# Second cross-attention of a Perceiver kernel: projection pieces between a step's halves, a second junk buffer, one head's side matrix added on GpSimd

## The chip, the cores and the metric

The kernel runs on one core of one Trainium2 chip. The metric is the time of one execution on the device in microseconds (us). Before the change it is 2459.25 us, the median of 3 runs (2456.62 to 2461.36). Everything is float32.

A core has five engines with a queue of instructions each: TensorE (PE; its weight loads are shown apart as PEld), VectorE (DVE), ScalarE (ACT), GpSimd (POOL) and SyncE (SP), which here only issues DMAs. They wait for one another through semaphores.

## The reference

The network has four layers; each is a cross-attention, a self-attention and a feed-forward part on a state `x` of 128 rows x 256. The four cross-attentions (called l0x, l1x, l2x, l3x in the kernel) read the same context of 12,544 rows x 256. Only the second, l1x, is touched. Cut to what matters, it is

```python
x = x + _L1_xattn_ref(ctx_1024, ctx_1024, _layernorm(x), fside_SxS2_0, fside_BxS2_0, ...)

def _L1_xattn_ref(K_in, V_in, Q_in, mask_attn, mask_pad, ...):      # 16 heads of 16
    K = K_in @ Wk + bk                                              # 12544 x 256
    V = V_in @ Wv + bv
    Q = Q_in @ Wq + bq                                              # 128 x 256
    KQ = einsum('bhld,bhpd->bhlp', K, Q) / sqrt(16)
    KQ = KQ + mask_pad.reshape(b, 1, l, 1)
    KQ = KQ + mask_attn.T.reshape(1, 1, l, lp)                      # 128 x 12544, the side matrix
    alpha = softmax(KQ, axis=2)                                     # over the 12544 keys
    O = einsum('bhlp,bhld->bhpd', alpha, V)
    return O.transpose(0, 2, 1, 3).reshape(b, lp, 256) @ Wo + bo
```

So each head needs the scores of 128 queries against 12,544 keys, with a full matrix added to them (the same for all heads), and then a softmax over the keys. The side matrix exists in l1x alone (`side=True` in the kernel).

## The kernel before, in words

**Projections.** Keys and values of all four cross-attentions are computed in small pieces: 512 keys by 128 features (`keys`, L200) or 256 keys by 256 features (`values`, L214), about four or eight weight loads each. A piece's products land in one PSUM bank (L315), are evicted by ScalarE (L209 for keys; L232 for values while l1x runs) and written to DRAM by a DMA that GpSimd issues (L212, L237). From there key and value tiles are fetched again. The pieces stand in one list in the order of layers; `pump(n)` (L142) issues the next n of them. While l1x runs, its own remaining pieces are issued, and then those of l2x.

**Cross-attention** (`cross`, L355). The 16 heads are worked off in 4 groups of 4; a group has 25 tiles of 512 keys (the last has 256), so there are 100 tiles in all. The softmax is exact, so each tile is visited twice. The first visit computes the scores with queries on the partitions (`score_s`, products L483) and only takes their maximum: for l1x, VectorE adds the side matrix and takes the maximum in one instruction (L491), which must also write its elementwise result somewhere; that goes to a buffer `junk` that nobody reads (L489, one buffer). A second short instruction reads the accumulator into `mxs`. When a group's 25 tiles are done, the maximum is folded into the queries (`raised`, `lower`; L505 to L515). The second visit, 27 steps later (`lead`, L364), computes the scores with keys on the partitions (`score_t`, products L533), VectorE adds the transposed side matrix into an SBUF tile `e` (L541), ScalarE takes the exponential in place (L546), and TensorE multiplies with the values (`values`, L572, products L588; a column of ones gives the softmax's denominator). VectorE adds this sum to `acc` (L592, L594).

**The order.** The order of l1x is written out by hand (`manual_schedule`, L615), in steps `at`. A step fetches key, value and side tiles, computes the scores (L623), issues pieces (L632 to L637) and then the weighted sum of the *previous* step's tile (L640 to L649). The scores of a step come in two halves (L561): first the maxima of heads 2 and 3 with the exponentials of heads 0 and 1, then the maxima of heads 0 and 1 with the exponentials of heads 2 and 3. Four heads use four separate row groups of the TensorE array, which is why the two kinds are mixed. Within a half all products are issued first and all drains after them: the maxima, then per head the add and the exponential. For steps 0 to 26 there are maxima alone, for 27 to 99 both, for 100 to 126 exponentials alone, then in one half with all four heads.

PSUM has 8 banks; each tile of scores, each piece and each weighted sum takes the next one in turn (`bank`, L135), and waits until whatever was in it eight allocations before is drained. `e` has two buffers.

How many pieces a step issues is set by a `goal` (l1x's own pieces have to be ready in time) and by `rate`, which for l1x is (0.95, 0.0, 1.2, 1.2, 0.4) pieces a step for steps 2 to 26, 27 to 51, 52 to 76, 77 to 101 and from 102 on. Own value pieces come on top, two in each of the steps up to 44.

Of the kernel before, what the change touches and what calls it, by code (L numbers as in the profile page):

```python
# [12 lines left out]
AF = mybir.ActivationFunctionType  # L13
ALU = mybir.AluOpType
# [4 lines left out]
P = 128  # L19
# [6 lines left out]
NST = -(-S2 // ST)  # L26
# [51 lines left out]
class Net:  # L78
# [276 lines left out]
    def cross(self, name, side=False, project=True, rate=()):  # L355
# [4 lines left out]
        nc, tc = self.nc, self.tc  # L360
# [6 lines left out]
        with ExitStack() as es:  # L367
# [18 lines left out]
            for u in range(units):  # L386
                g, r = width * u // 4, rows(u)
                q = pool.tile([P, P], F32, name=f"{name}_qb{u}", tag=f"qb{u}")
# [10 lines left out]
            kt, vt, ft, gt, mxs, es_, acc = {}, {}, {}, {}, {}, {}, {}  # L399
# [70 lines left out]
            def score_s(k, heads):  # L470

                u, i = divmod(k, NST)
                s, m = i * ST, min(ST, S2 - i * ST)
                if u not in mxs:
                    mxs[u] = pool.tile([P, width, NST], F32, name=f"{name}_mxs{u}", tag="mxs",
                                       bufs=2)
                t, at = kt[u, s // SB], s % SB
                banks = {j: self.bank(f"{name}_s{k}_{j}") for j in heads}

                def products():  # L480
                    for j in heads:
                        r = tile_of(u, j)
                        nc.tensor.matmul(banks[j][:, :m], qb[u][r, :], t[r, at : at + m],  # L483
                                         start=True, stop=True)

                def drain():
                    for j in heads:
                        if side:
                            junk = ep.tile([P, ST], F32, name=f"{name}_j{k}_{j}", tag="junk",  # L489
                                           bufs=1)  # L490
                            nc.vector.tensor_tensor_reduce(  # L491
                                out=junk[:, :m], in0=banks[j][:, :m], in1=ft[k][:, :m], scale=1.0,
                                scalar=-3.0e38, op0=ALU.add, op1=ALU.max,
                                accum_out=mxs[u][:, j, i : i + 1])
                        else:
                            nc.vector.tensor_reduce(out=mxs[u][:, j, i : i + 1],  # L496
                                                    in_=banks[j][:, :m], axis=AX.X, op=ALU.max)
                return products, drain
# [19 lines left out]
            def score_t(k, heads):  # L518

                u, i = divmod(k, NST)  # L520
                s, m = i * ST, min(ST, S2 - i * ST)
                t, at = kt[u, s // SB], s % SB
                banks = {j: self.bank(f"{name}_t{k}_{j}") for j in heads}
                if k not in es_:
                    es_[k] = ep.tile([P, width, ST], F32, name=f"{name}_e{k}", tag="e",
                                     bufs=5 if width == 2 else 2)
                e = es_[k]

                def products():
                    for a in range(m // P):  # L530
                        for j in heads:
                            r = tile_of(u, j)
                            nc.tensor.matmul(banks[j][:, a * P : (a + 1) * P],  # L533
                                             t[r, at + a * P : at + (a + 1) * P], qb[u][r, :],
                                             start=True, stop=True)

                def drain():
                    for j in heads:
                        src = banks[j][:, :m]
                        if side:  # L540
                            nc.vector.tensor_tensor(  # L541
                                out=e[:, j, :m], in0=src,
                                in1=gt[k][:, : m // P, :].rearrange("p a q -> p (a q)"),
                                op=ALU.add)
                            src = e[:, j, :m]
                        nc.scalar.activation(e[:, j, :m], src, AF.Exp)  # L546
                return products, drain

            def scores(ke, km):

                if ke is None and km is None:
                    return
                heads = tuple(range(width))
                if ke is None:
                    sets = [[(score_s, km, heads)]]
                elif km is None:
                    sets = [[(score_t, ke, heads)]]
                elif width == 2:
                    sets = [[(score_s, km, heads), (score_t, ke, heads)]]
                else:  # L560
                    sets = [[(score_s, km, (2, 3)), (score_t, ke, (0, 1))],  # L561
                            [(score_s, km, (0, 1)), (score_t, ke, (2, 3))]]
                for part in sets:
                    parts = [make(k, heads) for make, k, heads in part]
                    for products, _ in parts:
                        products()
                    for _, drain in parts:
                        drain()
                if km is not None:
                    raised(km)  # L570

            def values(ks):  # L572


                u, i = divmod(ks[0], NST)
                ps = self.bank(f"{name}_p{ks[0]}")
                todo = []
                for k in ks:
                    s = (k - u * NST) * ST
                    m = min(ST, S2 - s)  # L580
                    v, at, e = vt[u, s // SB], (s % SB) // P, es_.pop(k)
                    for a in range(m // P):
                        for j in range(width):
                            c = 17 * (width * (at + a) + j)
                            todo.append(((width * a + j) % 4, v[:, c : c + 32],
                                         e[:, j, a * P : (a + 1) * P]))
                for n, (c, lhs, rhs) in enumerate(todo):
                    nc.tensor.matmul(ps[32 * c : 32 * c + 32, :P], lhs, rhs, start=n < 4,  # L588
                                     stop=n >= len(todo) - 4, skip_group_check=True)
                if i == 0:  # L590
                    acc[u] = self.small.tile([P, P], F32, name=f"{name}_at{u}", tag="at")
                    nc.vector.tensor_copy(acc[u], ps[:, :P])  # L592
                else:
                    nc.vector.tensor_tensor(out=acc[u], in0=acc[u], in1=ps[:, :P], op=ALU.add)  # L594
# [20 lines left out]
            with tc.manual_schedule():  # L615
                for k in (0, 1):
                    fetch_k(k)
                for at in range(total + lead + 3):
                    fetch_k(at + 2)
                    fetch_v(at + 2 - lead)  # L620
                    ke = at - lead if 0 <= at - lead < total else None
                    km = at if at < total else None
                    scores(ke, km)  # L623
                    if 0 < at <= total and at % NST == 0:
                        lower(at // NST - 1)


                    left = sum(1 for (n, _, _), _ in self.jobs if n == name)
                    goal = min(n_k, 2 * (at + 6))
                    if at >= lead - 6:  # L630
                        goal = min(n_own, n_k + 2 * (at - lead + 7))
                    self.pump(min(left, max(0, goal - (n_own - left))))  # L632
                    phase = max(0, at - 2) // NST
                    due += rate[phase] if phase < len(rate) else 0.0
                    while due >= 1.0:
                        self.pump(1)
                        due -= 1.0  # L637


                    while waiting:  # L640
                        u, i = divmod(waiting[0], NST)
                        n = NST - i if NST - i < 2 * batch else batch
                        last = waiting[0] + n - 1
                        if ke is not None and ke - last < behind - batch + 1:
                            break
                        if last > waiting[-1]:
                            break
                        values(waiting[:n])
                        waiting = waiting[n:]  # L649
                    if ke is not None:  # L650
                        waiting.append(ke)
                    u, i = divmod(at - lead - 2 - NST, NST)
                    if i == 0 and 0 <= u < units:
                        finish(u)
# [826 lines left out]
```

## Time and profile before

| | us |
|---|---|
| median of 3 runs | 2459.25 (2456.62 to 2461.36) |
| the profiled execution | 2463.49 |
| its span, first to last instruction | 2461.6 |
| TensorE products busy | 2324.9 (94%) |
| weight loads busy | 1716.3 (70%) |
| VectorE busy | 1628.7 (66%) |
| ScalarE busy | 1150.0 (47%) |
| GpSimd busy | 246.2 (10%) |
| l1x, from its first score product to its last weighted sum | 648.0 to 1300.3 |

The profile shows one execution. A row of the timeline or of a group names the source line (L533), the engine, the operation, what it writes and reads ("l1x_t<-l1x_qb,l1x_kt"), and the shape; "x8" is how many instructions a row stands for, and in brackets stands how long the engine was idle before it and which engine's work ended that. Rows of the timeline begin with start and length in us. Matmuls are pipelined and their ends are modelled, so a TensorE that is busy 99% is not a TensorE at its peak. Each float32 product shows as two matmul records.

### The profile page before, as it was taken

Reading aid. Unit: us, or ns where it says so; the run is one execution under the profiler, and the core shown is the slowest. Engines: PE = TensorE matmul, PEld = TensorE weight load, DVE = VectorE, ACT = ScalarE, POOL = GpSimd, SP = SyncE. Lnnn points to the kernel's source line nnn. Section 1 sums busy time; section 2 is a strip of 40 time slices with the busy share of each in tenths; the row PEclk is TensorE's granted clock in tenths of the full one; section 3 lists DMA queues with packets and bytes.
Section 4 is the critical chain, followed back from the end, with each engine's and each line's share of the span. In section 5 each row is a group of like instructions: output and inputs, shape, how many; then the busy total and the mean of one; then the engine's idle time right before and its main releaser. Section 6 shows DMA issues by size and latency. Waiting matters only on the chain. (4 is left out here: it accounts for less than half of the span.)

```text
span 2461.6 us, 75645 instructions
## 1 busy us (share of the span) xinstructions
PE 2324.9 (94%) x32103; PEld 1716.3 (70%) x32103; DVE 1628.7 (66%) x3503; ACT 1150.0 (47%) x2109; POOL 246.2 (10%) x465
## 2 busy tenths in 40 slices
PE   6999999999899999999998998899999679999969
PEld 3358888876447876666777744478888546888848
DVE  2566688522477788888886734788882769888331
ACT  2213366773214445545582254046668302666832
POOL 2221100001221100000101111200000121000001
PEclk9999999999999999999999998999999888999979
DMA  7766633237779867777765675553322633333216
GB/s 273 263 222 215 208 97 93 69 118 278 259 232 303 275 216 223 229 227 219 223 198 191 211 254 195 165 151 92 92 78 68 231 109 101 91 91 97 63 44 225
DMA packets 191119, 430.29 MB, mean 175 GB/s; under 512 B 26908, under 2 KB 83248, under 8 KB 186688
## 3 DMA queue, kind: packets, MB, share of 16 engines
q1 hardware_dynamic: 154576, 269.26, 36.9%
q0 software_dynamic: 35840, 154.94, 16.8%
q8 instruction: 256, 4.19, 0.7%
q10 hardware_dynamic: 368, 1.25, 0.1%
q14 instruction: 79, 0.65, 0.1%
HBM read 319.18 MB, written 106.16 MB: 173 GB/s over the span
## 5 line engine op out<-in xcount | busy, mean ns | idle before, releaser
L546 ACT ACTIVATE l1x_e<-l1x_e 128x512 f32<-128x512 f32 (+1 forms) x400 | 240.5, 622 | 248.2 <-DVE l1x_e L541 248.2
L491 DVE CUSTOM_DVE_ANT_0 l1x_j<-l1x_s,l1x_f 128x512 f32<-128x512 f32 (+1 forms) x400 | 271.1, 678 | 80.9 <-PE l1x_t L533 29.9
L496 DVE TENSOR_REDUCE l0x_mxs<-l0x_s 128x1 f32<-128x512 f32 (+1 forms) x400 | 244.3, 672 | 97.5 <-PE l0x_s L483 66.0
L546 ACT ACTIVATE l0x_e<-l0x_t 128x512 f32<-128x512 f32 (+1 forms) x400 | 203.2, 594 | 176.9 <-PE l0x_t L533 173.4
L546 ACT ACTIVATE l3x_e<-l3x_t 128x512 f32<-128x512 f32 (+1 forms) x400 | 203.4, 594 | 167.2 <-PE l3x_s L483 92.6
L496 DVE TENSOR_REDUCE l2x_mxs<-l2x_s 128x1 f32<-128x512 f32 (+1 forms) x400 | 243.8, 672 | 36.7 <-PE l2x_t L533 24.3
L546 ACT ACTIVATE l2x_e<-l2x_t 128x512 f32<-128x512 f32 (+1 forms) x400 | 203.4, 594 | 137.2 <-PE l2x_t L533 133.5
L496 DVE TENSOR_REDUCE l3x_mxs<-l3x_s 128x1 f32<-128x512 f32 (+1 forms) x400 | 243.4, 671 | 33.1 <-PE l3x_t L533 23.9
L541 DVE TENSOR_TENSOR l1x_e<-l1x_t,l1x_g 128x512 f32<-128x512 f32 (+1 forms) x400 | 249.9, 671 | 11.3 <-PE l1x_t L533 8.3
L483 PE MATMUL l3x_s<-l3x_kt,l3x_qb 32*128 32x512 f32 (+1 forms) x800 | 202.8, 652 | 7.1 <-DMA l3x_kt<-l3x_kx 3.5
L533 PE MATMUL l1x_t<-l1x_qb,l1x_kt 32*128 32x128 f32 x3136 | 204.3, 284 | 2.7 <-ACT l1x_vs L232 0.6
L483 PE MATMUL l1x_s<-l1x_kt,l1x_qb 32*128 32x512 f32 (+1 forms) x800 | 203.2, 618 | 3.4 <-DMA l1x_kt<-l1x_kx 3.2
L533 PEld LDWEIGHTS l1x_t<-l1x_qb,l1x_kt 32*128 32x128 f32 x3136 | 171.6, 187 | 36.5 <-ACT l2x_ks L209 19.6
L483 PE MATMUL l2x_s<-l2x_kt,l2x_qb 32*128 32x512 f32 (+1 forms) x800 | 189.5, 620 | 5.8 <-DMA l2x_kt<-l2x_kx 5.3
L483 PE MATMUL l0x_s<-l0x_kt,l0x_qb 32*128 32x512 f32 (+1 forms) x800 | 183.5, 614 | 5.6 <-ACT l0x_ks L209 3.8
L533 PE MATMUL l3x_t<-l3x_qb,l3x_kt 32*128 32x128 f32 x3136 | 181.1, 281 | 0.0
L533 PE MATMUL l2x_t<-l2x_qb,l2x_kt 32*128 32x128 f32 x3136 | 180.0, 280 | 0.0
L533 PE MATMUL l0x_t<-l0x_qb,l0x_kt 32*128 32x128 f32 x3136 | 178.9, 279 | 0.0
L533 PEld LDWEIGHTS l3x_t<-l3x_qb,l3x_kt 32*128 32x128 f32 x3136 | 160.8, 187 | 6.5 <-issue 5.0
L533 PEld LDWEIGHTS l2x_t<-l2x_qb,l2x_kt 32*128 32x128 f32 x3136 | 159.8, 186 | 5.9 <-issue 5.0
L533 PEld LDWEIGHTS l0x_t<-l0x_qb,l0x_kt 32*128 32x128 f32 x3136 | 159.1, 186 | 5.9 <-issue 5.0
L588 PEld LDWEIGHTS l1x_p<-l1x_e,l1x_vt 128*32 128x32 f32 x3136 | 82.0, 110 | 51.3 <-DVE l1x_mxs L491 18.9
(599 smaller groups left out, 3665.8 us busy)
## 6 DMA issues: line engine op xcount, KB each, us to landing
l1x_f<-in_fside SPq DMA_DIRECT2D x96, 256.0 KB
l1x_g<-in_fsideT SPq DMA_DIRECT2D x96, 256.0 KB
w<-in_w_l3f POOLq DMA_DIRECT2D x16, 1024.0 KB, 5.1
l0x_vx<-l0x_vs POOLq DMA_DIRECT2D x24, 544.0 KB, 5.5
l0x_vt<-l0x_vx SPq DMA_DIRECT2D x48, 272.0 KB
l1x_vx<-l1x_vs POOLq DMA_DIRECT2D x24, 544.0 KB, 5.9
l1x_vt<-l1x_vx SPq DMA_DIRECT2D x48, 272.0 KB
l2x_vx<-l2x_vs POOLq DMA_DIRECT2D x24, 544.0 KB, 4.8
```

Of the source, the lines that this page charges most:

```text
L483: nc.tensor.matmul(banks[j][:, :m], qb[u][r, :], t[r, at : at + m], start=True, stop=True)
L491: nc.vector.tensor_tensor_reduce(out=junk[:, :m], in0=banks[j][:, :m], in1=ft[k][:, :m], scale=1.0, scalar=-3.0e38, op0=ALU.add, op1=ALU.m ...
L496: nc.vector.tensor_reduce(out=mxs[u][:, j, i : i + 1], in_=banks[j][:, :m], axis=AX.X, op=ALU.max)
L533: nc.tensor.matmul(banks[j][:, a * P : (a + 1) * P], t[r, at + a * P : at + (a + 1) * P], qb[u][r, :], start=True, stop=True)
L541: nc.vector.tensor_tensor(out=e[:, j, :m], in0=src, in1=gt[k][:, : m // P, :].rearrange("p a q -> p (a q)"), op=ALU.add)
L546: nc.scalar.activation(e[:, j, :m], src, AF.Exp)
L588: nc.tensor.matmul(ps[32 * c : 32 * c + 32, :P], lhs, rhs, start=n < 4, stop=n >= len(todo) - 4, skip_group_check=True)
```

## The change

Three things change in l1x. The unread output of the maxima gets two buffers in place of one. The pieces of a step are counted before the scores, and half of them, rounded up, is issued between the two halves of the scores, where a step has both kinds; the rest comes, as before, after the scores (now behind `lower`). And head 3's scores of the second visit no longer get their side matrix from VectorE: ScalarE copies them from PSUM to `e`, GpSimd adds the side matrix there in place, and the exponential is not issued with the others but by `last_head`, which is called after the first half of the next step (or after its only half), or at the latest before the weighted sum that reads it.

```diff
                             junk = ep.tile([P, ST], F32, name=f"{name}_j{k}_{j}", tag="junk",
-                                           bufs=1)
+                                           bufs=2)
...
                 def drain():
                     for j in heads:
                         src = banks[j][:, :m]
+                        if side and j == 3:
+                            part = e[:, j, :m]
+                            nc.scalar.copy(part, src)
+                            nc.gpsimd.tensor_tensor(
+                                out=part, in0=part,
+                                in1=gt[k][:, : m // P, :].rearrange("p a q -> p (a q)"),
+                                op=ALU.add)
+                            late[k] = part
+                            continue
                         if side:
                             nc.vector.tensor_tensor(
                                 out=e[:, j, :m], in0=src,
...
-            def scores(ke, km):
+            late = {}
+
+            def last_head(k):
+                part = late.pop(k, None)
+                if part is not None:
+                    nc.scalar.activation(part, part, AF.Exp)
+
+            def scores(ke, km, between):
...
-                for part in sets:
+                for n, part in enumerate(sets):
+                    if n == 1:
+                        between()
                     parts = [make(k, heads) for make, k, heads in part]
                     for products, _ in parts:
                         products()
                     for _, drain in parts:
                         drain()
+                    if n == 0 and ke is not None:
+                        last_head(ke - 1)
                 if km is not None:
                     raised(km)
...
                 u, i = divmod(ks[0], NST)
+                for k in ks:
+                    last_head(k)
                 ps = self.bank(f"{name}_p{ks[0]}")
...
-                    scores(ke, km)
-                    if 0 < at <= total and at % NST == 0:
-                        lower(at // NST - 1)
                     left = sum(1 for (n, _, _), _ in self.jobs if n == name)
                     goal = min(n_k, 2 * (at + 6))
                     if at >= lead - 6:
                         goal = min(n_own, n_k + 2 * (at - lead + 7))
-                    self.pump(min(left, max(0, goal - (n_own - left))))
                     phase = max(0, at - 2) // NST
                     due += rate[phase] if phase < len(rate) else 0.0
-                    while due >= 1.0:
-                        self.pump(1)
-                        due -= 1.0
+                    pieces = min(left, max(0, goal - (n_own - left))) + int(due)
+                    due -= int(due)
+                    inner = (pieces + 1) // 2 if side and ke is not None and km is not None else 0
+                    scores(ke, km, lambda: self.pump(inner))
+                    if 0 < at <= total and at % NST == 0:
+                        lower(at // NST - 1)
+                    self.pump(pieces - inner)
```

## The prediction

> **What bounds the kernel now.** I read the busy table by stage first, to see where the second attention (l1x) spends its time, then the timeline of two kinds of step, then the list of waits. Each step handles one 512-key tile; its start is read in the timeline as the first weight load of its products. The busy table, cut at step starts (columns: window, its length, busy time and count of TensorE products, weight loads, VectorE, ScalarE, GpSimd, then granted clock, DMA share, GB/s):
>
> ```profile
> core 0: us, PE busy (x) PEld busy (x) DVE busy (x) ACT busy (x) POOL busy (x), PEclk, DMA share, GB/s
> 647.98:750.63 102.65, 96.56 (x390) 47.85 (x391) 75.02 (x219) 18.20 (x29) 22.96 (x35) 0.97 0.75 244
> ...
> 765.78:877.62 111.84, 111.84 (x1413) 94.06 (x1409) 86.26 (x208) 53.80 (x95) 15.54 (x32) 1.00 0.84 268
> 877.62:913.17 35.55, 35.06 (x502) 26.74 (x498) 32.71 (x88) 16.00 (x27) 1.72 (x3) 0.95 0.70 216
> 913.17:1212.03 298.86, 297.26 (x3681) 193.82 (x3677) 254.55 (x640) 149.43 (x252) 17.04 (x33) 0.99 0.72 224
> 1212.03:1296.63 84.60, 82.66 (x1735) 65.50 (x1732) 69.52 (x136) 68.10 (x118) 6.05 (x13) 1.00 0.62 196
> ```
>
> Row 1 is maxima only (27 steps), rows 2 to 4 both passes (16 steps with two pieces, 7 with one or none, 48 with one or two), row 5 the exponential pass alone (26). No engine is free by much: in row 4 VectorE is 85% busy, in row 5 VectorE and ScalarE are 82% and 80% busy. The order decides. A one-piece step of row 4 in the timeline:
>
> ```profile
> 1002.24 0.70 PE L483 MATMUL l1x_s<-l1x_kt,l1x_qb 32*128 32x512 f32 x2
> ...
> 1003.00 0.67 ACT L209 ACTIVATE l2x_ks<-l2x_k,cols 128x512 f32<-128x512 f32 x1
> ...
> 1003.40 0.69 DVE L491 CUSTOM_DVE_ANT_0 l1x_j<-l1x_s,l1x_f 128x512 f32<-128x512 f32 x1 [0.73 <-PE l1x_t L533]
> ...
> 1004.24 0.69 DVE L491 CUSTOM_DVE_ANT_0 l1x_j<-l1x_s,l1x_f 128x512 f32<-128x512 f32 x1
> ...
> 1004.86 1.28 DVE L541 TENSOR_TENSOR l1x_e<-l1x_t,l1x_g 128x512 f32<-128x512 f32 x2
> ...
> 1005.58 1.23 ACT L546 ACTIVATE l1x_e<-l1x_e 128x512 f32<-128x512 f32 x2 [1.91 <-DVE l1x_e L541]
> ...
> 1007.74 0.70 PE L483 MATMUL l1x_s<-l1x_kt,l1x_qb 32*128 32x512 f32 x2
> ```
>
> See the pitches: two maxima start 0.84 apart, but a maximum and the add behind it 0.62 apart. The 0.22 is the second maximum waiting for the first to release the single junk buffer (in the built program its wait names the accumulator read just ahead of it). VectorE's step is 2(0.84+0.62+0.60+0.60)+0.2 = 5.5 us; the row's steps average 298.86/48 = 6.23. What is lost beside it is seen in the waits of this row:
>
> ```profile
> PEld l1x_t L533 <- ACT l2x_ks L209: 19.6, 30, 0.9
> ```
>
> The key piece's eviction stands in ScalarE's queue behind the exponentials, and the next step's second half waits for that PSUM bank. A stretch of row 5, the exponential pass alone:
>
> ```profile
> 1287.15 1.17 PE L533 MATMUL l1x_t<-l1x_qb,l1x_kt 32*128 32x128 f32 x32
> ...
> 1288.40 2.48 DVE L541 TENSOR_TENSOR l1x_e<-l1x_t,l1x_g 128x512 f32<-128x512 f32 x4 [0.82 <-PE l1x_t L533]
> 1289.13 2.42 ACT L546 ACTIVATE l1x_e<-l1x_e 128x512 f32<-128x512 f32 x4 [0.67 <-DVE l1x_e L541]
> 1289.27 1.17 PE L533 MATMUL l1x_t<-l1x_qb,l1x_kt 32*128 32x128 f32 x32
> ...
> 1291.60 0.79 PEld L588 LDWEIGHTS l1x_p<-l1x_e,l1x_vt 128*32 128x32 f32 x26 [0.46 <-ACT l1x_e L546]
> ...
> 1292.59 1.17 PE L533 MATMUL l1x_t<-l1x_qb,l1x_kt 32*128 32x128 f32 x32
> ```
>
> The next tile's scores (1289.27) are issued before this tile's exponentials are done, so TensorE, VectorE and ScalarE work on different tiles at once: 84.60/26 = 3.25 us a step.
>
> **The change, part by part.** *Second junk buffer.* The 0.22 goes: a pair of maxima in each half-step, three gaps in a maxima-only step. In row 1 the maxima run back to back at 0.84, 3.36 us a step, and the waits of 650 to 704 us put 11.4 and 6.4 us of weight-load waits on the maxima. TensorE's own one-piece step there is 1.14+1.98 less 0.14 overlap = 2.98. At most the 15 steps from 650.2 to 704.0 us, now 3.59 long, fall to that (9 us); the key tiles' DMA waits and a DMA share of 0.75 take part back. I take -5, bounds -9 and 0.
>
> *Pieces between the halves.* The first half's evictions get time and the piece's eviction comes earlier in ScalarE's queue, so the L209 wait goes. The price: two halves no longer overlap. Together they take 2.03 unstalled; apart about 1.14 each less 0.07, so +0.18 (bounds 0 and 0.3). Two-piece steps of row 2 alternate 6.62 and 7.36 (mean 6.99); without the stall 6.62+0.18 = 6.80: 16 x -0.19 = -3. VectorE (5.5 less 0.44 for the gaps and 0.60 for head 3's add: 4.5) and the DMAs fit.
>
> *Head 3.* VectorE loses one add (0.60) a step, ScalarE gains a copy (0.55 from the L232 copies' pitch), GpSimd an add. ScalarE mixes copies and exponentials without table loads today. The GpSimd add has no near row: its only two-input add, 128x64, took 315 ns; scaled by elements that is 2.5 us, while memsets (206 ns for 128 columns, 978 for 1024) give 0.5 as floor. [...] But it has cover. In a one-piece step the second half starts at 2.98 us, its first maximum at 4.14, the second and the add 0.62 each later, head 2's exponential at 6.10, head 3's copy at 6.70 to 7.3; its result is called for at 10.3, in the next step (worked out below). So 3.0 us are free, more than either value; above 3.0 it would show.
>
> *Where head 3's exponential stands.* This decides. It is queued on ScalarE in the **next** step: behind the exponentials of heads 0 and 1 of that step, and, where the exponential pass is alone, behind heads 0, 1, 2 and the copy of head 3. The weighted sum (L588 before) of the old tile comes at the end of that same step on TensorE, and its fourth product waits for it. Behind that product stand the rest of the sum and all scores of the step after. So TensorE can no longer start step n+1 before ScalarE has worked through step n: a closed loop.
>
> Loop with both passes: scores to first maximum 1.16 (1002.24 to 1003.40); two maxima 1.24; add to exponential 0.72; three exponentials 0.60+0.60+0.63; to the sum 0.05; rest of the sum to the next scores 0.99 (1291.60 to 1292.59). Together 5.99 us, whether the step has one piece or none. With two, TensorE itself reaches the sum at about 6.0 us and doesn't wait: 6.80.
> Row 3: 7 x 5.99 less 0.2 for the short tile = 41.7 against 35.55: +6.
> Row 4: 38 x 5.99 + 10 x 6.80 + 1 for the two group changes = 296.6 against 298.86: -2. What the relief of VectorE gains is eaten by the loop.
>
> Loop of the exponential pass alone: 1.25 to the first add, 0.73 to the exponential, three exponentials 1.80, copy 0.55, last exponential 0.63, 0.05, rest of the sum 0.99: 6.00 against 3.25. A piece there (1.91) lies inside the wait. 26 x 6.00 less 0.8 for the short tile = 155.2 against 84.60: **+70.6**. The last tile is exposed at the end, with its GpSimd add: +2.
>
> Sum: -5 -3 +6 -2 +70.6 +2 = +69. The profiled execution took 2463.49 us (span 2461.6, 1.9 around it); with the change 2532. The median is 4.2 lower: 2459.25 + 69 = **2528 us**. The other stages keep their work.
>
> **Rivals.**
> *Faster: no loop.* If the late exponential came in time, both-pass steps would fall to TensorE's floor: one piece 2.03+1.98+1.08 less two overlaps of 0.07, and 0.18 for the split: 5.13; so row 4 becomes 38 x 5.13 + 68 + 1 = 264 (-35), row 3 7 x 4.5 = 31.5 (-4), row 5 ScalarE's 4 x 0.60 + 0.55 + a piece's copy in two steps of five (0.23) = 3.2 (-1); with -5 and -3 that is -48: 2411. For it speak VectorE's 85% and the L209 wait. Against it: the exponential would have to end within 4.0 us of a step's start (1.1 where the pass is alone), and the durations above give 4.95 and 4.96.
> *Loop only at the end.* With both passes the chain may be shorter than added up (a step of 5.3 instead of 5.99): 45 x -0.7 = -31: 2497. For it: three of its terms are pitches of back-to-back instructions. Against: the 1.16 and 0.72 are read off directly.
> *GpSimd too slow.* If its add takes 4.0 us, or waits behind a DMA issue in its queue, 38 one-piece steps grow by 1.0: 2566. For it: no row of that size. Against: both values lie below 3.0.
>
> **How the numbers follow.** Chances: my forecast 0.73, loop only at the end 0.10, slow GpSimd 0.12, no loop 0.05. 0.2% (5 us) is about what a measurement of this kernel can tell from no change. Slower: the first three but for a sliver, 0.93; same 0.02; faster 0.05. Range: the forecast's bounds (row 1 -4 to +5, row 2 -3 to +3, the two loops 0.3 a step over 71 steps) give 2505 to 2552; taking in the second rival's near half and part of the third's, 2500 to 2560.
>
> **What the profile after would show.** The maxima 0.62 apart in both places; L209 and L232 no longer named by the second half's weight loads; the fourth product of the weighted sum waiting on ScalarE's late exponential and starting 5.0 us after the step's first product, in every step but the two-piece ones; steps of 6.0 us from about 1210 on, with TensorE idle nearly half of them; that stage near 155 us. Wrong would be: steps near 3.3 there (no loop), or GpSimd's add as the last thing waited for.

## The result, and the profile after

The changed kernel takes 2546.23 us (median of 4 runs, 2543.98 to 2556.55); the kernel before took 2458.07 us beside it (4 runs, 2456.62 to 2461.36). The ratio is 1.0365 (95% interval 1.0333 to 1.0396): 3.7% slower. The forecast was 2528 us with a range of 2500 to 2560.

The profiled span grew from 2461.6 to 2546.3 us, by 84.7. The second attention, l1x, from its first score product to its last weighted sum, grew from 652.6 (648.0 to 1300.6) to 739.3 us, by 86.7; the stages around it give 2 back. So the whole loss is in l1x. Here is the forecast beside the measured times, in the stages of the prediction's rows (row 1 reaches here up to the start of row 2, so that it holds, behind the 27 steps with maxima alone, two steps with both passes):

| us | row 1, maxima | row 2, two pieces | row 3, one or none | row 4, both passes | row 5, exponentials alone | tail | sum |
|---|---|---|---|---|---|---|---|
| before | 117.80 | 111.84 | 35.56 | 298.85 | 84.61 | 3.98 | 652.6 |
| forecast | 112.8 | 108.8 | 41.7 | 296.6 | 155.2 | 6 | 721.1 |
| after | 112.92 | 113.05 | 44.37 | 292.07 | 169.93 | 6.96 | 739.3 |

The busy table of the changed kernel, rows 3, 4 and 5 of these stages (columns: window, its length, busy time and count of TensorE product records, weight loads, VectorE, ScalarE, GpSimd, granted clock, DMA share, GB/s):

```profile
874.84:919.21 44.37, 32.49 (x503) 25.73 (x499) 31.09 (x87) 20.02 (x38) 10.57 (x10) 0.84 0.57 180
919.21:1211.28 292.07, 279.17 (x3677) 183.39 (x3676) 221.09 (x584) 166.82 (x297) 77.77 (x82) 0.99 0.73 229
1211.28:1381.21 169.93, 112.50 (x1736) 85.26 (x1732) 56.57 (x110) 79.19 (x144) 39.16 (x41) 0.81 0.32 100
```

The last row has doubled, and no engine in it is near its capacity: TensorE is busy 66% of it, ScalarE 47%, VectorE 33%, GpSimd 23%. TensorE's 1736 product records (two for each product) are as many as before (1735) but are shown busy for 112.5 us instead of 82.7, at a granted clock of 0.81 instead of 1.00. In row 4 VectorE went from 85% to 76% busy, and the stage is only 2% shorter.

A one-piece step of row 4 (timeline; only the links of the path are shown):

```profile
1005.96 0.70 PE L483 MATMUL l1x_s<-l1x_kt,l1x_qb 32*128 32x512 f32 x2
...
1007.11 0.69 DVE L491 CUSTOM_DVE_ANT_0 l1x_j<-l1x_s,l1x_f 128x512 f32<-128x512 f32 x1 [0.76 <-PE l1x_t L533]
...
1007.73 0.69 DVE L491 CUSTOM_DVE_ANT_0 l1x_j<-l1x_s,l1x_f 128x512 f32<-128x512 f32 x1
...
1008.34 1.28 DVE L552 TENSOR_TENSOR l1x_e<-l1x_t,l1x_g 128x512 f32<-128x512 f32 x2
...
1009.06 1.23 ACT L557 ACTIVATE l1x_e<-l1x_e 128x512 f32<-128x512 f32 x2 [1.77 <-DVE l1x_e L552]
...
1010.20 0.61 ACT L565 ACTIVATE l1x_e<-l1x_e 128x512 f32<-128x512 f32 x1
...
1010.86 1.06 PE L612 MATMUL l1x_p<-l1x_e,l1x_vt 128*32 128x128 f32 x26 [0.37 <-ACT l1x_e L565]
...
1011.85 0.70 PE L483 MATMUL l1x_s<-l1x_kt,l1x_qb 32*128 32x512 f32 x2
```

This is the closed loop of the forecast, link by link. The two maxima are now 0.62 apart, not 0.84. Then the adds, two exponentials, head 3's late exponential (L565, of the *previous* tile) at 1010.20, the rest of that tile's weighted sum (L612) at once behind it, and the next step's scores behind that: 5.89 us. The forecast had 5.99.

Two steps of row 5, where the exponential pass is alone; the first starts at 1259.66, the second at 1266.36, the third at 1273.97:

```profile
1259.66 1.17 PE L533 MATMUL l1x_t<-l1x_qb,l1x_kt 32*128 32x128 f32 x32
...
1261.63 1.82 ACT L557 ACTIVATE l1x_e<-l1x_e 128x512 f32<-128x512 f32 x3 [2.54 <-DVE l1x_e L552]
...
1263.83 0.63 ACT L565 ACTIVATE l1x_e<-l1x_e 128x512 f32<-128x512 f32 x1
...
1264.51 1.92 PE L612 MATMUL l1x_p<-l1x_e,l1x_vt 128*32 128x128 f32 x26 [3.33 <-ACT l1x_e L565]
...
1266.36 2.09 PE L533 MATMUL l1x_t<-l1x_qb,l1x_kt 32*128 32x128 f32 x32
...
1268.52 1.89 DVE L552 TENSOR_TENSOR l1x_e<-l1x_t,l1x_g 128x512 f32<-128x512 f32 x3 [1.77 <-PE l1x_t L533]
...
1272.13 1.91 PE L612 MATMUL l1x_p<-l1x_e,l1x_vt 128*32 128x128 f32 x26 [3.10 <-ACT l1x_e L565]
...
1273.97 2.09 PE L533 MATMUL l1x_t<-l1x_qb,l1x_kt 32*128 32x128 f32 x32
```

Again the sum's rest waits for L565, and the next scores come behind the sum. But something is in it that the forecast didn't have. The same 32 records of score products take 1.17 us in the first step and 2.09 in the second, and the same 26 records of the sum take 1.92 us (1.06 in row 4's step above). The engine's rows of exactly these two steps, in the columns of the first table, say why:

```profile
1259.66:1266.36 6.70, 3.37 (x66) 2.49 (x65) 2.17 (x4) 2.83 (x5) 1.27 (x1) 0.80 0.15 43
1266.36:1273.97 7.61, 4.51 (x65) 3.33 (x65) 2.17 (x4) 2.83 (x5) 1.27 (x1) 0.50 0.26 71
```

The granted TensorE clock is 0.50 throughout the second step. Cut at its own changes, the clock around these steps reads:

```profile
1250.10:1256.90 6.80, 5.85 (x63) 4.77 (x64) 2.13 (x4) 2.01 (x4) 1.26 (x1) 0.50 0.47 140
1256.90:1263.70 6.80, 3.84 (x75) 2.60 (x73) 2.22 (x5) 4.26 (x9) 1.42 (x2) 1.00 0.37 134
1263.70:1277.40 13.70, 9.79 (x125) 7.66 (x126) 3.73 (x8) 4.12 (x8) 2.54 (x2) 0.50 0.22 60
```

In row 5 every stretch at half clock lasts 3.4 us or a multiple of it (6.8, 13.7). In the list of waits of row 5 (engine and line, what it waited for: us in total, times, longest) one line stands for nearly all that TensorE waits, the weight loads of the sum in each of the 26 steps:

```profile
PEld l1x_p L612 <- ACT l1x_e L565: 65.0, 26, 3.6
```

These waits differ. In the 14 steps in which TensorE has no projection piece to do, neither products nor weight loads run for 3.1 to 3.3 us; in the 12 steps with a piece for 0.2 to 1.4 us. Every stretch at half clock begins in a step without a piece, between 2.0 us into its wait and 0.5 us behind the end. A step with a piece is long (up to 6.8 us) where it begins in such a stretch.

### The profile page after: what moved, and what is told of

Its sections match the earlier page's. It is cut to its first block, busy times and chain, and to the rows that moved or that the text cites. A ratio compares the mean times of both kernels' runs of the same rounds, so it can differ in the third digit from the quotient of the medians.

```text
span 2546.3 us, 75819 instructions
## 1 busy us (share of the span) xinstructions
PE 2329.5 (91%) x32103; PEld 1719.7 (68%) x32103; DVE 1560.9 (61%) x3403; ACT 1189.2 (47%) x2209; POOL 371.1 (15%) x565
## 3 DMA queue, kind: packets, MB, share of 16 engines
q10 hardware_dynamic: 368, 1.25, 0.1%
## 5 line engine op out<-in xcount | busy, mean ns | idle before, releaser
L491 DVE CUSTOM_DVE_ANT_0 l1x_j<-l1x_s,l1x_f 128x512 f32<-128x512 f32 (+1 forms) x400 | 253.4, 677 | 122.1 <-PE l1x_t L533 83.9
L557 ACT ACTIVATE l1x_e<-l1x_e 128x512 f32<-128x512 f32 x300 | 181.9, 621 | 297.5 <-DVE l1x_e L552 297.3
L612 PE MATMUL l1x_p<-l1x_e,l1x_vt 128*32 128x128 f32 x3136 | 146.4, 295 | 84.2 <-ACT l1x_e L565 84.1
L533 PE MATMUL l1x_t<-l1x_qb,l1x_kt 32*128 32x128 f32 x3136 | 211.8, 304 | 0.0
L552 DVE TENSOR_TENSOR l1x_e<-l1x_t,l1x_g 128x512 f32<-128x512 f32 x300 | 191.5, 673 | 32.5 <-PE l1x_t L533 31.6
L612 PEld LDWEIGHTS l1x_p<-l1x_e,l1x_vt 128*32 128x32 f32 x3136 | 96.4, 115 | 129.9 <-ACT l1x_e L565 103.5
L533 PEld LDWEIGHTS l1x_t<-l1x_qb,l1x_kt 32*128 32x128 f32 x3136 | 178.5, 206 | 8.2 <-issue 7.2
L545 POOL TENSOR_TENSOR l1x_e<-l1x_e,l1x_g 128x512 f32<-128x512 f32 (+1 forms) x100 | 124.5, 1245 | 353.9 <-ACT l1x_e L544 346.6
```

The costliest lines, as they stand in the source:

```text
L491: nc.vector.tensor_tensor_reduce(out=junk[:, :m], in0=banks[j][:, :m], in1=ft[k][:, :m], scale=1.0, scalar=-3.0e38, op0=ALU.add, op1=ALU.m ...
L533: nc.tensor.matmul(banks[j][:, a * P : (a + 1) * P], t[r, at + a * P : at + (a + 1) * P], qb[u][r, :], start=True, stop=True)
L545: nc.gpsimd.tensor_tensor(out=part, in0=part, in1=gt[k][:, : m // P, :].rearrange("p a q -> p (a q)"), op=ALU.add)
L552: nc.vector.tensor_tensor(out=e[:, j, :m], in0=src, in1=gt[k][:, : m // P, :].rearrange("p a q -> p (a q)"), op=ALU.add)
```

## The experiments

The changed kernel differs from the one before in three parts and in one place in a queue. The theory of the forecast is that the place of head 3's exponential closes a loop from ScalarE through the weighted sum to the next scores; its main rival is that GpSimd's add is too slow. A second question came with the profile: why row 5 is 14.7 us longer than the loop's terms. The times to compare with are 2459.13 us of the kernel before for the first four runs, 2461.62 for the last four. All diffs but those of e5 are against the changed kernel. Here is where the time of l1x went in each of them (us, in the stages of the first table):

| | row 1 | row 2 | row 3 | row 4 | row 5 | tail | sum |
|---|---|---|---|---|---|---|---|
| before | 117.80 | 111.84 | 35.56 | 298.85 | 84.61 | 3.98 | 652.6 |
| after | 112.92 | 113.05 | 44.37 | 292.07 | 169.93 | 6.96 | 739.3 |
| e1, exponential earlier | 112.77 | 113.05 | 35.05 | 281.84 | 104.48 | 7.44 | 654.6 |
| e2, no head 3 | 115.50 | 113.05 | 33.39 | 276.91 | 83.73 | 3.98 | 626.6 |
| e3, waits filled | 111.91 | 113.05 | 42.27 | 296.71 | 150.17 | 7.86 | 722.0 |
| e4, head 3 with both passes | 112.98 | 113.05 | 43.78 | 297.21 | 85.41 | 3.98 | 656.4 |
| e5, two junk buffers | 113.02 | 108.14 | 33.35 | 285.36 | 83.70 | 3.98 | 627.6 |
| e6, pieces between | 115.26 | 113.05 | 37.19 | 283.75 | 83.85 | 3.98 | 637.1 |
| e7, head 3 alone | 116.47 | 111.30 | 47.05 | 304.08 | 169.64 | 8.36 | 756.9 |
| e8, all pieces between | 115.49 | 109.89 | 33.96 | 276.00 | 83.71 | 3.98 | 623.0 |

Rows with the same code in different kernels differ by some us from one profiled execution to the next: row 4 of the changed kernel, of e3 and of e4 is the same program, and took 292.07, 296.71 and 297.21 us. Nearly all of this is one step, the first with a value piece of l2x: it takes 6.49, 10.52 and 11.58 us, and without it the three rows are 285.6, 286.2 and 285.6 us. In the long ones TensorE waits for the piece's context rows; in e4's step, from 1166.49 us on,

```profile
PE l2x_v L315 <- DMA l2x_cv<-in_ctxT: 2.7, 1, 2.7
```

and the piece then takes 3.75 us instead of 1.97. The step is as long in e1, e2, e6 and e8 (11.3 to 13.6 us), and short in the kernel before, e5 and e7 (7.08, 6.74, 6.28). So it is long where pieces stand between the halves, except in the profile of the changed kernel itself, where the DMA had all but landed. Whether it belongs to that part of the change stays open; where row 4 is compared, 4 to 7 us have to be allowed for it.

**e1: the late exponential, placed earlier in ScalarE's queue.** Everything of the change stays; only the call is issued ahead of the step's own drains instead of behind them.

```diff
                     for products, _ in parts:
                         products()
-                    for _, drain in parts:
-                        drain()
                     if n == 0 and ke is not None:
                         last_head(ke - 1)
+                    for _, drain in parts:
+                        drain()
```

> One edit on the changed kernel: head 3's late exponential is issued at the front of the next step's ScalarE work, ahead of that step's exponentials, instead of behind them. GpSimd's add, the copy and every other instruction stay. Loop theory (its place in ScalarE's queue makes the wait): one-piece steps with both passes fall from 5.90 to TensorE's 5.15, and where the exponential pass is alone ScalarE now stands still for GpSimd (1.25 plus hand-overs), about 4.4 us a step against 6.5 changed and 3.25 before. By stages against before: -5 (maxima), +1 (two pieces), -3 (none), -31 (one or two), +30 (alone), +3 (end): 2453 us. Rival, that the copy on ScalarE and the add on GpSimd themselves are what costs: they are all still there, so it stays at 2520 or above.

Measured: 2460.58 us, ratio 1.0007 (0.9988 to 1.0027), as long as the kernel before. Row 5 fell from 169.93 to 104.48 us. A step of it in the timeline:

```profile
1256.39 1.17 PE L533 MATMUL l1x_t<-l1x_qb,l1x_kt 32*128 32x128 f32 x32
...
1256.82 0.56 ACT L544 COPY l1x_e<-l1x_t 128x512 f32<-128x512 f32 x1
1257.47 1.26 POOL L545 TENSOR_TENSOR l1x_e<-l1x_e,l1x_g 128x512 f32<-128x512 f32 x1 [2.08 <-ACT l1x_e L544]
...
1258.76 0.63 ACT L565 ACTIVATE l1x_e<-l1x_e 128x512 f32<-128x512 f32 x1 [1.38 <-POOL l1x_e L545]
...
1259.30 1.65 ACT L557 ACTIVATE l1x_e<-l1x_e 128x512 f32<-128x512 f32 x3
...
1260.43 1.17 PE L533 MATMUL l1x_t<-l1x_qb,l1x_kt 32*128 32x128 f32 x32
```

The copy is done, GpSimd adds in 1.26 us, and ScalarE, whose next instruction is L565, stands idle for 1.38 us; then come the three other exponentials, and then the next copy. That is a smaller ring, between ScalarE and GpSimd alone: 0.65 to the add, 1.29 to the late exponential, 0.54 to the others, 1.56 to the next copy (at 1260.86): 4.04 us. Now TensorE doesn't wait for a whole step of ScalarE, and its scores of the next tile start while the exponentials run. What follows: moving one ScalarE instruction per tile, with every duration left as it was, gives back 86 us of the 88 lost. So the place in the queue is the cause, and GpSimd's speed is not, in the changed kernel. In e1 it is: each step of row 5 is 0.8 us longer than in e2, where VectorE does the add. Against its own expectation e1 is 8 us long: row 5 grew by 20 us over the kernel before instead of 30, but row 4 fell by 17 instead of 31. Of these 14, 5 are the late DMA; the rest lies in steps of 5.3 to 5.7 and 7.3 to 7.7 us, where 5.15 and 7.07 were expected, and was not followed up.

**e2: the change without head 3.**

```diff
-                        if side and j == 3:
+                        if False:
```

> The changed kernel with head 3 left on VectorE as before: second junk buffer and pieces between the halves alone. Loop theory: nothing closes a loop; one-piece steps are set by TensorE (1.11 + 1.92 + 1.10 + 1.01 = 5.14) or VectorE (5.1), two-piece steps 7.07 as in the changed kernel, the exponential pass alone 3.25 as before. -5, +1, 0, -26 to -32, 0: 2422 to 2428 us. Rival, that splitting halves and pieces costs TensorE more than it gains: 2458 or above.

Measured: 2436.94 us, ratio 0.9899 (0.9865 to 0.9932): 1.0% faster than before, not quite as much as expected. Row 5 is what it was (83.73 us), row 4 is 22 us shorter than before (27 to 28, as expected, if the step with the late DMA is left out of both). So the other two parts gain, and head 3 costs 109 us on top of them (2546.23 - 2436.94), not 88: part of its cost was paid with the gain of the rest. Of the 109, 86 are the place of its exponential (e1), and 24 stay when that is moved.

**e3: TensorE's waits in row 5 filled.** The loop stays closed. Ahead of each weighted sum of that stage TensorE gets one or three products whose results are overwritten, on operands that lie ready.

```diff
                 ps = self.bank(f"{name}_p{ks[0]}")
+                if side and ks[0] >= 73:
+                    for _ in range(1 if pieces else 3):
+                        nc.tensor.matmul(ps, self.ident, self.cst[:, 0:512], start=True, stop=True)
```

> The changed kernel with extra work: in the exponential pass alone (tiles 73 on) three products of 128x512 with the identity (one where the step has a piece) are written into the weighted sum's own bank ahead of the sum, which overwrites them; the output is the same. They lie in TensorE's wait for the late exponential. Clock theory (the wait lets TensorE's clock fall, so that half the steps have products of 2.09 instead of 1.17 us): granted clock near 1.0 there, all steps near the 5.84 us of those with the full clock, the stage 170 down to 152: 2528 us in spite of more work. Rival, that the long steps have another cause (GpSimd, PSUM banks, DMA): 2546 or more.

Measured: 2533.16 us, ratio 1.0293 (1.0252 to 1.0335). TensorE has more to do, and the kernel is 13 us *shorter*; row 5 is 19.8 us shorter (in the profile, row 4 has the long step with the late DMA). Its busy row and one of its steps:

```profile
1211.95:1362.12 150.17, 135.90 (x1842) 85.66 (x1838) 56.56 (x109) 79.22 (x144) 39.22 (x41) 1.00 0.36 113
```

```profile
1286.14 1.17 PE L533 MATMUL l1x_t<-l1x_qb,l1x_kt 32*128 32x128 f32 x32
1287.25 2.84 PE L603 MATMUL l1x_p<-cst 128*128 128x512 f32 x6
...
1290.99 1.06 PE L615 MATMUL l1x_p<-l1x_e,l1x_vt 128*32 128x128 f32 x26 [0.56 <-ACT l1x_e L565]
1291.98 0.73 PE L533 MATMUL l1x_t<-l1x_qb,l1x_kt 32*128 32x128 f32 x16
```

The granted clock is 1.00 for the whole stage, the score products take 1.17 us again and the sum's rest 1.06, and the steps are 5.84 us: the loop at full clock. So the changed kernel's row 5 is two things: 26 x 5.84 less the short tile, about 150 us, is the loop; the 20 us beyond it is TensorE's clock, which fell because of the loop's waits.

**e4: head 3 on GpSimd only where both passes run.**

```diff
-                        if side and j == 3:
+                        if side and j == 3 and k < total - lead:
```

> The changed kernel, but tiles 73 to 99 (the exponential pass alone) have head 3 on VectorE as before; tiles 0 to 72 as changed. Loop theory priced by stage: the stage alone goes back from 170 to about 85 us and the tail of 3 us goes, the both-pass stages keep their +1, +9 and -7: 2458 us, the time of before, so that the whole loss sits in the 26 steps. Rival, that the loss is spread over all 100 tiles (a copy and an add for each): three quarters stay, 2524.

Measured: 2464.21 us, ratio 1.0014 (0.9999 to 1.0029): no difference from before that is clear of noise. Against e2, which differs from it in head 3 alone, it is 27 us longer by the medians, and its l1x 30 us in the profile: rows 3 and 4 grow by 10 and 20. So the loop costs time with both passes too, 0.4 to 1.5 us a step. Against the kernel before it looks free there, because the second junk buffer and the moved pieces gain about as much in the same steps.

**e5: the second junk buffer alone** (against the kernel before).

```diff
                             junk = ep.tile([P, ST], F32, name=f"{name}_j{k}_{j}", tag="junk",
-                                           bufs=1)
+                                           bufs=2)
```

> The kernel before with the second junk buffer alone. The 0.22 us between two maxima goes everywhere: -5 where there are maxima alone, and VectorE's step with both passes falls from 5.5 to 5.1 while the piece's eviction still stands behind the exponentials. If VectorE's length sets those steps, up to 48 x 0.4 = -19 more (2435); if the L209 wait sets them, nothing more (2454). I expect between, 2445.

Measured: 2441.65 us, ratio 0.9917 (0.9884 to 0.9951). Row 1 is 4.8 us shorter, row 2 3.7, row 4 13.5. The two-piece steps alternate between 6.63 and 6.89 us instead of 6.63 and 7.36: of the 0.73 us by which every other one was long, 0.47 was the junk buffer.

**e6: the pieces between the halves alone.** Without head 3 as in e2, and one junk buffer.

```diff
-                                           bufs=2)
+                                           bufs=1)
...
-                        if side and j == 3:
+                        if False:
```

> The kernel before with the pieces between the halves alone (one junk buffer, head 3 on VectorE). The wait for the key piece's eviction goes, VectorE's 5.5 us stays: one-piece steps 5.5, two-piece 7.07, so 38 x 5.5 + 10 x 7.07 + 1 = 281 against 299, +1 in the steps with two own pieces, nothing elsewhere: 2442. If the two small parts are independent, this and the second junk buffer alone together give the -22 of both.

Measured: 2451.05 us, ratio 0.9949 (0.9932 to 0.9967): a gain, but half of what was expected. In the profile it is in row 4 (-15 us) and in the last two steps of row 1 (-3), where both passes run; the two-piece steps of row 2 take 7.07 us each, as in e2. By the medians the two parts don't quite add: e5 gains 20 us and e6 10.6, both together (e2) 22, though the intervals are too wide to decide it. Row 2 shows one reason: where the pieces lie between the halves, the second junk buffer changes nothing (113.05 us with either), since TensorE's own order has become the longer path there.

**e7: head 3 alone.** One junk buffer, all pieces behind the scores as before.

```diff
-                                           bufs=2)
+                                           bufs=1)
...
-                    inner = (pieces + 1) // 2 if side and ke is not None and km is not None else 0
+                    inner = 0
```

> The kernel before with head 3's part alone (copy, GpSimd add, late exponential; one junk buffer, all pieces behind the scores). Loop theory: the loop does not need the other two parts. One-piece steps 5.90 + 0.22 = 6.12, two-piece 6.6 to 6.8, the pass alone 6.54, the tail 3: +3 -4 +10 +85 +3 = 2555. Rival, that the pieces between the halves are part of the loss: clearly below the changed kernel's 2546, 2500.

Measured: 2573.78 us, ratio 1.0453 (1.0415 to 1.0492), a miss by 19 us, to the slow side. One-piece steps take 6.13 us, where the loop with a junk wait put back gives 6.12, and row 5 grew by 85 us, both as expected. Of the 19 us the profile puts 7 in l1x: two-piece steps, some of which take 7.23 to 7.34 us instead of 6.6 to 6.8, row 3 (47.05 us), and the tail. Another 4 lie in the stages around l1x, and the rest is no more than the spread between executions of one kernel (2450.4 to 2472.6 us for the one before).

**e8: all pieces between the halves, no head 3.** A step's pieces follow one another on TensorE instead of standing in two places.

```diff
-                        if side and j == 3:
+                        if False:
...
-                    inner = (pieces + 1) // 2 if side and ke is not None and km is not None else 0
+                    inner = pieces if side and ke is not None and km is not None else 0
```

> Second junk buffer and head 3 on VectorE, and all pieces of a step between the halves instead of half of them. In the changed kernel a two-piece step took 7.07 where 6.80 was predicted: 0.25 for the split halves and 0.20 for pulling the two pieces apart. If that 0.20 is the price of a switch of products on TensorE, two-piece steps take 6.87: 26 x -0.20 = -5 against 2437 with half of them: 2432. Rival, that the second piece's eviction then stalls a bank: 2437 or more.

Measured: 2428.74 us (4 runs, 2422.54 to 2434.26), ratio 0.9856 (0.9819 to 0.9892): 1.4% faster than the kernel before, and the fastest version here. Here are TensorE's rows of the pieces (L315) in a two-piece step, of the changed kernel and then of e8:

```profile
791.16 1.99 PE L315 MATMUL l1x_v<-l1x_kvw,l1x_cv 128*128 128x256 f32 x8
793.08 0.70 PE L483 MATMUL l1x_s<-l1x_kt,l1x_qb 32*128 32x512 f32 x2
...
794.18 1.99 PE L315 MATMUL l1x_v<-l1x_kvw,l1x_cv 128*128 128x256 f32 x8
796.11 1.08 PE L612 MATMUL l1x_p<-l1x_e,l1x_vt 128*32 128x128 f32 x32
```

```profile
793.83 3.72 PE L315 MATMUL l1x_v<-l1x_kvw,l1x_cv 128*128 128x256 f32 x16
797.48 0.70 PE L483 MATMUL l1x_s<-l1x_kt,l1x_qb 32*128 32x512 f32 x2
```

In both the profile shows no gap between TensorE's rows. Apart, the two pieces take from 791.16 to 793.08 and from 794.18 to 796.11, 3.85 us together; side by side 3.65 (793.83 to 797.48). The steps around them begin at 790.05 and 797.12, and at 792.73 and 799.59: 7.07 and 6.86 us. So separating two pieces costs 0.20 us.

One question was not tried on the chip: opening the loop by taking the weighted sum a further step later. That needs a third buffer of `e`, 8 KB a partition (4 x 512 values of 4 bytes).

## Why the prediction was right, and where its sizes were off

The direction, the cause and the stage are those of the forecast; the time is 18.2 us above it, inside the range. In the table above, after less forecast is +0.1, +4.3, +2.7, -4.5, +14.7 and +1.0 us by row: +18.2. That the first is so small is luck (next paragraph), and the +14.7 is 19.8 too little for the clock and 5 too much for the loop. (The bounds that the forecast lists add up to 2500 to 2557 if all fall the same way, not to 2505 to 2552; its range holds nearly all of that.)

*Second junk buffer, -5.* The maxima are 0.62 apart, as forecast, but row 1's -4.9 is this number by luck. The 27 steps with maxima alone took 102.65 us before and take 101.01 now; two-buffer kernels lie between 100.0 (e5) and 103.8 us (e8) there, one-buffer ones between 101.4 (e7) and 103.1 (e6). Single steps do fall to 2.99 us, but from about 650 to 704 us the weight-load waits on the maxima only went from 11.4 and 6.4 us to 10.1 and 5.9, and VectorE's waits for the side tiles' DMA rose from 0.5 to 7.9 us. The other 3.2 us came in the two steps with both passes behind them, before and after:

```profile
750.63:765.78 15.15, 14.54 (x138) 11.35 (x137) 10.12 (x24) 8.38 (x13) 1.37 (x4) 0.89 1.06 327
749.88:761.79 11.91, 11.91 (x137) 9.26 (x137) 8.76 (x22) 7.83 (x13) 2.71 (x5) 1.00 1.04 322
```

There either small part shortens them (13.03 us in e5, 12.14 in e6). For the buffer by itself -5 is too small: it gains 20 us by the medians (e5), and 13.5 of the 25 us that its profile shows in l1x are in row 4. The forecast had this relief "eaten by the loop", and in the changed kernel it is: e5 and e2 show the gain there, and e4 that the loop takes it.

*Pieces between the halves, -3.* This step failed: row 2 got 1.2 us longer instead of 3 shorter. The step that was wrong is "6.62+0.18 = 6.80". The split of the halves is 0.25 (e8's 6.87 less the 6.62), and a term was missing: the change puts one piece between the halves and one behind, and the separation of the pieces costs another 0.20 (7.07). Sixteen steps by 0.27 is the 4.3 us. That the key piece's eviction no longer holds up the second half is right: in e6 row 4 gains 15 us.

*Head 3.* For GpSimd's add the forecast had 0.5 us as floor and 2.5 from the scaled 128x64 add. The groups of instructions of the changed kernel give it (out<-in, shape, count, then busy us and mean ns, idle time before it and what ended it):

```profile
L545 POOL TENSOR_TENSOR l1x_e<-l1x_e,l1x_g 128x512 f32<-128x512 f32 (+1 forms) x100 | 124.5, 1245 | 353.9 <-ACT l1x_e L544 346.6
```

1.245 us is the mean of all 100, and 1.267 that of the 96 whole tiles, half of what the scaling gave. The add lies under the cover, which was forecast at 3.0 us and is 2.9 in most one-piece steps (from the end of the copy to the start of L565): TensorE waits for L565, and L565 follows on ScalarE's own work. The profile shows it waiting for GpSimd only once, 2.7 us at the last tile, which the forecast had priced (+2). What that +2 takes for the add itself, no run shows; in the profile the last add, of 128x256, took 0.71 us, from 1386.33 on, behind a memset on GpSimd that began only when a DMA of `l2x_vs` had landed (1386.22), and the tail grew by 3.0 us (3.98 to 6.96).

*Where head 3's exponential stands.* Right, and shown by e1, which moves only this. Both-pass steps: 5.99 forecast, 5.89 to 5.90 measured; from the first exponential to the sum's rest it took 1.80 us (1009.06 to 1010.86) instead of the 1.88 of three pitches added up. In row 4 this makes 38 x 0.09 = 3.4 of the 4.5 us gained against the forecast; in e3 and e4 these steps take 5.90 us too, and their row 4 came out at the forecast only because of the step with the late DMA. Pass alone: forecast 6.00, at full clock 5.84 (e3), but 6.54 on average in the changed kernel (169.93/26).

*The term that was mis-sized* is therefore "rest of the sum 0.99" and "1.25 to the first add", taken from a stage in which TensorE ran at full clock and applied to one in which its products wait 57.4 of 169.93 us for L565. In the step at half clock they are 1.84 (1272.13 to 1273.97) and 2.16 (1266.36 to 1268.52), together 1.76 more, which is the difference between 7.61 and 5.84. The granted clock throughout that step is 0.50. The length of the wait does not tell where it falls: all 14 long waits are 3.1 to 3.3 us, and 12 of them have half clock in them or right behind them while two, in the steps from 1226.49 and 1315.26, leave it at 1.00. So steps of 5.84 and of 7.6 us stand side by side, and what decides between them is not shown. The forecast wrote "TensorE idle nearly half" of these steps and did not price that. An estimate from the two kinds of step, all at 5.84 or all at 7.61 us, is 151 to 197 us for the row, and 169.93 lies within. Row 3, where several steps issue no piece, has it too: clock 0.84, 44.37 us instead of 41.7.

*The rivals.* "No loop" fell, since the profile shows TensorE waiting for L565 in all 26 steps of row 5 and in 34 of row 4; and its price of 2411 us is not reached where the loop is open either (e1 2460.58, e2 2436.94, e8 2428.74). "Loop only at the end" fell: both-pass steps are 5.90, not 5.3. "GpSimd too slow" fell with 1.245 us, and with e1.

Still open is what the remaining 0.26 us of every second two-piece step in e5 is, and why the clock falls in some steps of row 5 and not in others. (e6's profiled execution, 2445.9 us, is the shortest of its 11, and e5's, 2448.42, one of the longer of its 6: stage times of these two stand for one execution each.)

## What to carry to other kernels

Before an instruction is put off to a later place in an in-order queue, walk once round: what must end before it there, what waits for it, and what stands behind that waiter; if the way comes back to the same queue one step later, the step is the length of that ring, however little each engine has to do (here 3.25 us became 5.84). Price such a ring with the clock that TensorE will have while it waits (here 0.81 on average instead of 1.00), not with the durations of a full stage. And measure the parts of a change alone as well as together: here 22 us that two parts gain together hid the 27 us that the third costs with both passes.

## What the runs showed of the hardware that was not expected

Adding products made the kernel faster: one or three more per tile in TensorE's waits (e3) brought the stage from 169.93 to 150.17 us, because the granted clock stayed at 1.00 instead of 0.81 on average. With TensorE waits of 3.1 to 3.3 us in 14 of 26 steps it was 0.50 for 3.4 to 13.7 us at a time, steps with short waits included; with waits of 0.6 us (up to 1.2 in the first step) it stayed at 1.00. And the order of TensorE's work has a price with no wait in it that the profile shows: 0.20 us for two projection pieces that stand apart instead of together, 0.25 for two halves of scores that stand apart.
